# Two chained attention layers on one core: the output projection of layer 0 as seven block products into x1^T

## The chip, the cores and the metric

The kernel runs on one core of one Trainium2 chip. The metric is device time in microseconds (us) of one launch; lower is better. All data are fp32.

## The reference, cut to what matters

The input x is (8, 32, 32, 256): 8 batches of 1024 tokens with 256 channels. Layer 0 is attention with 4 heads, whose output projection is added to its input; layer 1 is a gated attention with one head of 32 channels on the result x1.

```python
# layer 0
q, k, v = split(xf @ W_qkv)                      # per head, 256 channels each
atten = softmax(einsum('bihd,bjhd->bijh', q, k) * C ** -0.5, axis=2)
res = einsum('bijh,bjhd->bihd', atten, v)        # heads side by side
x1 = res @ W_out + b_out + xf
# layer 1
f, g, h = x1 @ Wf + bf, x1 @ Wg + bg, x1 @ Wh + bh
b = softmax(einsum('bik,bjk->bij', g, f), axis=-1)
y = gamma * einsum('bij,bjd->bid', b, h) + x1
```

## The kernel before

**Algebra.** For each head the weights are folded once (`fold_weights`, L293): Wqk = Wq Wk^T and Wvo = Wv Wout, so that scores are (x Wqk) x^T and the head's contribution is softmax(..) x Wvo. The softmax is not shifted; the sum of the exponentials is divided out after the projection.

**Seven block products.** Most products are done as a 2 by 2 block scheme with seven instead of eight block products (`seven`, L234). It takes sums of blocks as operands, made by VectorE ahead (`sum_a` L204, `sum_b` L214), and uses three PSUM banks x, y, z in three tasks. `one` issues products 1, 6, 5 into x, y, z, ScalarE copies x to a tile e, and VectorE makes u = y + e. `two` adds product 2 to x and 7 to y; ScalarE takes result 11 from x, VectorE makes v = y + e and result 22 = z + v. `three` adds product 4 to y and 3 to z; VectorE makes results 21 = y + e and 12 = z + u. The adds are all on L264, the matmuls all on L247. In the trace the banks are `psx`, `psy`, `psz`, with `_q` for the queries and `_y` for the weighted values.

**Steps.** The work is a list of steps (L891), each a unit (a batch and head of layer 0, or a batch of layer 1) and one of two halves of 512 query columns. With batch b > 0, layer 1 of batch b-1 stands after head 1 of batch b; for the last batch it stands after head 3. The body of a step (L917 to L989) is a list of tasks, each with a place: `put(tasks, *places)`. The tasks are sorted by place, and this order is the program order of TensorE, VectorE and ScalarE (L870, a manual schedule): each engine takes its instructions strictly in that order. A layer-0 step i does

- its own scores (`scores`, L524): two groups of three tasks at places 0, 2, 4 and 6, 8, 10, exp on ScalarE;
- of step i-1: block sums of the exponentials (`sums`, L559, four operations of 128x1024 on VectorE), the column sums for the denominators (`first` and `second` in L582 to L600, a GpSimd all-reduce and two small DMAs that turn a row into columns), and the first two tasks of the weighted values (`products`, L608; places 5 and 9);
- of step i-2: the third task of the weighted values (place 1), `invert` (L604) and `project` (L629) at places 3 and 7;
- in the second half, the next head's queries (`queries`, L496) and their four block sums.

**The projection before** (`project`, L629) takes for each half eight matmuls of 128x128 by 128x256: the stationary operand is y (128 tokens at a time), the moving one is Wvo. The result has tokens in partitions, so that one VectorE operation multiplies by the inverse denominator (one number per partition) and adds to the rows of x1 (`rows1`, L648).

**Around it.** `residual` (L425) starts `rows1` as x + b_out on VectorE. Layer 1 needs x1 transposed: `turn_rows` (L357) moves 32x32 squares with DMAs on the queue of SyncE (SP) and transposes each square on VectorE (L382, L385); it does so for x of the next batch and for x1. For the last batch x1 is transposed by TensorE (`transpose_rows`, L342, called at L986). `queries_apart` (L687) makes f and g of layer 1 and spreads copies of them by DMAs from SP. `values` (L723) makes the value rows of layer 1 in four tasks, whose PSUM banks (pool `psm`, two buffers) VectorE empties (L729). After the last step the code from L1012 on finishes layer 1 of the last batch.

**Pools** (L866): `rows` has 4 buffers, `xT` 2, `m0` 1, `ps` six banks, `psm` two.

Of the kernel before, what the change touches and what calls it, by code (L numbers as in the profile page):

```python
# [16 lines left out]
P = 128  # L17
# [3 lines left out]
def kernel(  # L21
# [14 lines left out]
):  # L36

# [111 lines left out]
    bout_sb = const.tile([P, C], F32, tag="bout", name="bout_sb")  # L149
# [8 lines left out]
    def load_rest():  # L158
        with nc.allow_non_contiguous_dma(reason="small bias vectors, loaded once"):
            nc.sync.dma_start(bout_sb, b_out.partition_broadcast(P))  # L160
# [20 lines left out]
    wblocks = {}  # L181
# [52 lines left out]
    def seven(name, width, parts, matmuls, outs, tags, copy, after=None):  # L234
# [7 lines left out]
        def bank(k):  # L242
            banks[k] = tile_of("ps", [P, NB], f"ps{k}_{name}")[:, :width]
# [22 lines left out]
        def one():  # L266
            for k, number in (("x", 1), ("y", 6), ("z", 5)):
                bank(k)
                product(k, number, True)
            nc.scalar.copy(scratch("e"), banks["x"])  # L270
            add(shaped(scratch("u")), "y", sbs["e"])
# [19 lines left out]
    NARROW = dict(e="eh", u="uh", v="w")  # L291

    def fold_weights(h):  # L293
# [20 lines left out]
        def multiply(i, what):  # L314
# [13 lines left out]
            if i == 0:  # L328
# [4 lines left out]
                wblocks[h] = b_operands(blocks, sums)  # L333

# [22 lines left out]
    def turn_rows(b, src, dst, layer, scratch=None):  # L357

        Q = 32

        def end():
            if b not in dst:
                dst[b] = tile_of("xT", [P, CC, N], f"x{layer}T_{b}")
            return dst[b]

        def flat(t):
            return t.rearrange("p u n -> p (u n)").rearrange("p (s q) -> p s q", q=P)  # L370

        def move(a, c=None):
            to, rows_v = flat(end() if scratch is None else scratch()), flat(src[b])
            if c is not None:
                to, rows_v = to[:, ts(c, NT), :], rows_v[:, c::CC, :]
            for q in range(P // Q):
                nc.sync.dma_start(to[ts(q, Q), :, ts(a, Q)], rows_v[ts(a, Q), :, ts(q, Q)])

        def piece(k, c):
            to = end()[:, c, ts(k, NB)]  # L380
            if scratch is None:
                nc.vector.transpose(to, to)  # L382
            else:
                squares = scratch()[:, k, :].rearrange("p (t c q) -> p t c q", c=CC, q=P)
                nc.vector.transpose(to.rearrange("p (t q) -> p t q", q=P), squares[:, :, c, :])  # L385

        return (
            [partial(move, a, c) for a in range(P // Q)
             for c in ((None,) if scratch else range(CC))],
            [partial(piece, k, c) for k in range(NBLK) for c in range(CC)],  # L390
        )

# [32 lines left out]
    def residual(b):  # L425


        def piece(i):
            if i == 0:
                rows1[b] = tile_of("rows", [P, NT, C], f"x1_{b}")  # L430
            nc.vector.tensor_tensor(
                rows1[b][:, ts(i, 2), :], rows[b][:, ts(i, 2), :],
                bout_sb.unsqueeze(1).broadcast_to([P, 2, C]), ALU.add,
            )

        return [partial(piece, i) for i in range(NT // 2)]
# [40 lines left out]
    def values_tile(name):  # L477
        v = tile_of("v", [P, NT, CV], name)
        nc.gpsimd.memset(v[:, :, C : C + 1], 1.0)
        return v  # L480


    class Layer0:
        def __init__(self, b, h):
            self.b, self.h, self.name = b, h, f"{b}_{h}"
            self.p, self.y, self.r = {}, {}, {}
            self.products_of, self.pblocks = {}, {}
# [8 lines left out]
        def queries(self):  # L496
# [6 lines left out]
            def after():  # L503
                t = tile_of("qs", [P, 3, NBLK, HB], f"qs_{self.name}")
                q = self.q.rearrange("p c (k e i) -> p c e k i", k=NBLK, e=2)
                blocks = [q[:, c, e] for c in range(CC) for e in range(2)]
                sums = [blocks[1]] + [t[:, k] for k in range(3)]
                self.pieces = sum_b(sums, *blocks)
                self.blocks = b_operands(blocks, sums)

            def piece(k):
                self.pieces[k]()  # L512

# [7 lines left out]
                WIDE, nc.scalar.copy, after,  # L521
            ), [partial(piece, k) for k in range(4)]

        def scores(self, blk):  # L524
# [10 lines left out]
            for g in range(0, half, 2):  # L535
# [3 lines left out]
                def after(g=g, out=out):  # L539
# [8 lines left out]
                         self.blocks[number][:, blk, :])  # L548
# [10 lines left out]
        def sums(self, blk):  # L559
# [6 lines left out]
            def start():  # L566
# [4 lines left out]
                s2 = tile_of("s2", [P, half, HB], f"s2_{n}")  # L571
                s3 = tile_of("s3", [P, half, HB], f"s3_{n}")
                sums = [t[:, 1], s2, s3, t[:, 0]]
# [8 lines left out]
            def first():  # L582
                t = made["t"]
                made["m"] = m = tile_of("m0", [P, 2, 2, HB], f"m_{n}")
                tt(m, t[:, :, 0:2, :], t[:, :, 2:4, :], ALU.add)

            def second():
                m = made["m"]
                r = tile_of("rs", [P, 2, HB], f"rs_{n}")
                tt(r, m[:, :, 0, :], m[:, :, 1, :], ALU.add)  # L590
                tt(r[:, 0, :], r[:, 0, :], r[:, 1, :], ALU.add)  # L591
                t = tile_of("rb", [P, NB], f"rb_{n}")
# [9 lines left out]
            return [partial(piece, i) for i in range(4)], [first, second]  # L602

        def invert(self, blk):  # L604
            n = self.first + blk * HT
            nc.vector.reciprocal(inverse[:, n : n + HT], self.r[blk])
# [22 lines left out]
        def project(self, blk):  # L629

            b = self.b
# [501 lines left out]
```

## Time and profile before

| | |
|---|---|
| median of 3 runs | 2338.45 us (2338.1 to 2339.13) |
| profiled execution, its own time | 2338.61 us |
| its span, first to last instruction | 2336.7 us |
| TensorE matmuls, time in which one was under way | 2326.9 us |
| VectorE busy | 1481.7 us |
| ScalarE busy | 522.5 us |
| GpSimd busy | 211.5 us |
| data moved by DMA | 42.94 MB |
| granted TensorE clock | 0.999 |

Each fp32 matmul has two records in the trace, and records overlap: the mean record lasts 379 ns, but 16 records of the same kind take 3.47 us from the first's start to the next group's. VectorE records overlap as well, by less than a tenth of a microsecond. So lengths of stretches are best read from one start to the next.

### The profile page before, as it was taken

The page shows a single profiled execution, that of the slowest core. Times are in us where ns is not written, and L with a number is a line of the kernel's source. Part 1 is how long each engine was busy: PE and PEld are TensorE (multiplying, and loading weights), DVE is VectorE, ACT ScalarE, POOL GpSimd, SP SyncE. Part 2 cuts the span into 40 slices and gives each one's busy share as a digit, 9 for nine tenths or more (in the row PEclk, how much of TensorE's full clock was granted, in tenths as well). Part 3 has the DMA queues.
Part 4 walks back from the last instruction along what each step waited for, and adds up shares of the span by engine and source line. Part 5 has one row for each costly group of instructions (what it writes and reads, how often), then busy time and mean ns, then how long its engine had stood idle before and what let it go on. Part 6 is the DMA issues. An engine that isn't in the chain of part 4 may idle for free.

```text
span 2336.7 us, 26026 instructions
## 1 busy us (share of the span) xinstructions
PE 2326.9 (100%) x10394; PEld 1918.8 (82%) x10394; DVE 1481.7 (63%) x2398; ACT 522.5 (22%) x875; POOL 211.5 (9%) x79
## 2 busy tenths in 40 slices
PE   9999999999999999999999999999999999999999
PEld 7888888788878888788887888878888788888877
DVE  6667775377754767557774577645776457766635
ACT  2222222222221222212222122221222222222222
POOL 0111111011110111101111011110011101101110
PEclk9999999999999999999999999999999999999999
DMA  4000010100101001110011000110001100000100
GB/s 138 1 1 1 1 37 14 34 1 11 27 17 32 1 19 21 19 29 1 19 26 18 24 1 19 30 18 19 1 19 30 19 19 1 1 1 1 30 7 31
DMA packets 170257, 42.94 MB, mean 18 GB/s; under 512 B 158160, under 2 KB 163024, under 8 KB 170128
## 3 DMA queue, kind: packets, MB, share of 16 engines
q1 hardware_dynamic: 170128, 41.20, 8.0%
q8 instruction: 84, 1.38, 0.3%
q14 instruction: 45, 0.37, 0.1%
HBM read 13.37 MB, written 8.52 MB: 9 GB/s over the span
## 4 chain that ended last, share of the span: by engine, by line
PE 99%; DVE 1%; DMA 0%; issue 0%; ACT 0%
PE psy_y L247 14%; PE psy L247 14%; PE psx L247 9%; PE pa_l L834 9%; PE po L637 9%; PE psx_y L247 9%; PE psz_y L247 9%; PE psz L247 9%; PE psy_q L247 4%; PE psx_q L247 2%; PE psz_q L247 2%; PE pr_v_l L466 2%; PE ps_l L746 1%; PE pm_fg L703 1%; PE pwqk L318 0%; PE pwvo L318 0%
## 5 line engine op out<-in xcount | busy, mean ns | idle before, releaser
L593 POOL PARTITION_ALL_REDUCE rb<-rs x64 | 206.9, 3233 | 2046.6 <-DVE rs L591 2019.8
L247 PE MATMUL psx<-q,x0T 128*128 128x256 f32 x1024 | 263.6, 380 | 0.0
L247 PE MATMUL psy<-qs,xs 128*128 128x256 f32 x1024 | 263.0, 379 | 0.0
L247 PE MATMUL psz<-q,xs 128*128 128x256 f32 x1024 | 262.8, 379 | 0.0
L541 ACT ACTIVATE p<-p 128x1024 f32<-128x1024 f32 x128 | 135.3, 1057 | 554.8 <-DVE p L264 554.8
L247 PE MATMUL psy_y<-s,xt 128*128 128x256 f32 x1024 | 242.4, 380 | 0.1
L637 PE MATMUL po<-wvo,y 128*128 128x256 f32 x1024 | 241.9, 379 | 0.0
L247 PE MATMUL psx_y<-p,x 128*128 128x256 f32 x1024 | 241.9, 379 | 0.0
L834 PE MATMUL pa_l<-v_l,s_l 128*128 128x257 f32 x1024 | 232.1, 381 | 0.4 <-DVE v_l L729 0.4
L247 PEld LDWEIGHTS psx<-q,x0T 128*128 128x128 f32 x1024 | 194.0, 190 | 45.2 <-issue 21.0
L637 PEld LDWEIGHTS po<-wvo,y 128*128 128x128 f32 x1024 | 194.6, 190 | 39.5 <-issue 14.8
L834 PEld LDWEIGHTS pa_l<-v_l,s_l 128*128 128x128 f32 x1024 | 193.8, 190 | 36.6 <-issue 10.5
L247 PEld LDWEIGHTS psx_y<-p,x 128*128 128x128 f32 x1024 | 194.7, 190 | 34.0 <-issue 8.6
L247 PEld LDWEIGHTS psy_y<-s,xt 128*128 128x128 f32 x1024 | 191.9, 190 | 30.6 <-issue 2.4
L247 PEld LDWEIGHTS psy<-qs,xs 128*128 128x128 f32 x1024 | 194.5, 190 | 27.0 <-DVE qs L512 0.4
L247 PEld LDWEIGHTS psz<-q,xs 128*128 128x128 f32 x1024 | 194.7, 190 | 26.3
L264 DVE TENSOR_TENSOR u<-psy,e 128x512 f32<-128x512 f32 x128 | 88.4, 691 | 144.3 <-ACT e L270 73.4
L276 ACT ACTIVATE p<-psx 128x512 f32<-128x512 f32 x128 | 76.4, 597 | 413.7 <-PE psx L247 413.6
L264 DVE TENSOR_TENSOR v<-psy,e 128x512 f32<-128x512 f32 x128 | 87.8, 686 | 124.5 <-PE psy L247 124.5
L247 PE MATMUL psy<-qs,x0T 128*128 128x256 f32 x512 | 131.6, 380 | 0.7 <-DVE v L264 0.7
L648 DVE SCALAR_TENSOR_TENSOR x<-po,inverse,x 128x256 f32<-128x256 f32 x256 | 111.9, 478 | 31.3 <-PE po L637 22.4
L270 ACT COPY e<-psx 128x512 f32<-128x512 f32 x128 | 73.8, 576 | 257.8 <-PE psx L247 257.8
(120 smaller groups left out, 2839.8 us busy)
## 6 DMA issues: line engine op xcount, KB each, us to landing
out_dram<-x SPq DMA_DIRECT2D x15, 512.0 KB, 2.6
x<-in_x_dram SPq DMA_DIRECT2D x14, 512.0 KB, 4.6
x0T<-x SPq DMA_DIRECT2D x224, 32.0 KB, 1.9
fg<-x SPq DMA_DIRECT2D x112, 64.0 KB, 2.1
fg<-fg SPq DMA_DIRECT2D x56, 64.0 KB, 2.0
w<-in_L_conv_W_qkv_dram SPq DMA_DIRECT2D x4, 512.0 KB, 7.3
x<-in_x_dram SPq DMA_DIRECT2D x4, 256.0 KB, 4.8
w<-in_L_conv_W_qkv_dram SPq DMA_DIRECT2D x4, 256.0 KB, 6.4
```

The costliest lines, as they stand in the source:

```text
L247: nc.tensor.matmul(banks[k][:, ts(i, w)], lhsT=lhsT, rhs=rhs, start=first and n == 0, stop=True, skip_group_check=True,)
L264: nc.vector.tensor_tensor(dst, shaped(banks[k]), shaped(other), ALU.add)
L270: nc.scalar.copy(scratch("e"), banks["x"])
L276: copy(outs["11"](), shaped(banks["x"]))
L466: nc.tensor.matmul(pm[:, ts(j, C)], lhsT=src()[:, c, ts(2 * t2 + j, P)], rhs=w()[:, c, :], start=(c == 0), stop=(c == CC - 1),)
L541: exp(both, both)
L593: nc.gpsimd.partition_all_reduce(t, r.rearrange("p e i -> p (e i)"), P, bass_isa.ReduceOp.add)
L637: nc.tensor.matmul(pm[:, ts(j, C)], lhsT=self.y[blk][:, c, ts(2 * t2 + j, P)], rhs=folded[self.h][1][:, c, :], start=(c == 0), stop=(c == ...
L648: nc.vector.scalar_tensor_tensor(acc, pm[:, ts(j, C)], inverse[:, n : n + 1], acc, ALU.mult, ALU.add)
L703: nc.tensor.matmul(pm[ts(k, half)], lhsT=w[:, c, :], rhs=x1T_of[b][:, c, ts(k, NB)], start=(c == 0), stop=(c == CC - 1),)
L746: nc.tensor.matmul(pm, lhsT=self.f[ts(r, CK), ts(j0 + r, P)], rhs=self.g[ts(r, CK), ts(blk, NB)], start=True, stop=True,)
L834: nc.tensor.matmul(pm[:, : C + 1], lhsT=p[:, j, ts(ti, P)], rhs=v[:, j, : C + 1], start=(j == 0), stop=(j == NT - 1),)
```

## The change

The projection now computes Wvo^T times y^T, so that its result is x1 transposed, in seven block products of the same size (128x128 by 128x256) in the three tasks of `seven`. Its PSUM comes from the two `psm` banks (y and z share one). The denominators now lie along the free axis: `invert` writes its columns to DRAM as a row and reads that back into all partitions, and one VectorE operation multiplies the whole 128x1024 result by it. A DMA of GpSimd's queue then adds the product to x1^T in SBUF. x1^T starts as x^T + b_out, made by ScalarE. Rows of x1, needed for layer 1's output, are made from x1^T by 32x32 squares (`turn_back`), for all batches; TensorE's 16 transposes of the last batch go. The block sums of the queries are made per half. The key sums of the exponentials are in place, without the tiles s2 and s3. The next batch's squares are moved over two steps and transposed one step earlier than before. In the last step the queries of layer 1 move behind the last step, and the values there are spread between other products.

```diff
-    def seven(name, width, parts, matmuls, outs, tags, copy, after=None):
+    def seven(name, width, parts, matmuls, outs, tags, copy, after=None, two_banks=False):
...
         def bank(k):
-            banks[k] = tile_of("ps", [P, NB], f"ps{k}_{name}")[:, :width]
+            if not two_banks:
+                banks[k] = tile_of("ps", [P, NB], f"ps{k}_{name}")[:, :width]
+            elif k == "z":
+                banks[k] = banks["y z"][:, width : 2 * width]
+            else:
+                t = tile_of("psm", [P, NB], f"ps{k}_{name}")
+                banks["y z"], banks[k] = t, t[:, :width]
...
     def fold_weights(h):
...
+            else:
+                t4 = const.tile([P, 4, P], F32, tag=f"wo{h}", name=f"wo{h}")
+                sums = [t4[:, k, :] for k in range(4)]
+                blocks = [t[:, c, ts(e, P)] for e in range(CC) for c in range(CC)]
+                run(sum_a(sums, *blocks))
+                oblocks[h] = a_operands(blocks, sums)
...
+    def squares(dst, src, swap):
...
+        def move(a, c):
+            for q in range(P // Q):
+                to, rows_v = dst(), src()
+                if swap:
+                    nc.sync.dma_start(
+                        to[ts(q, Q), :, c, ts(a, Q)], rows_v[ts(a, Q), c, :, ts(q, Q)]
+                    )
...
+        def piece(k):
+            to = dst()
+            n = to.shape[1] * to.shape[2] // 4
+            flat = to.rearrange("p u v i -> p (u v) i")[:, ts(k, n), :]
+            nc.vector.transpose(flat, flat)
...
+    def turn_back(b):
...
+        return squares(end, lambda: x1T_of[b].rearrange("p c (n i) -> p c n i", i=P), True)
...
     def residual(b):
...
+        def piece(c):
+            if c == 0:
+                x1T_of[b] = tile_of("xT", [P, CC, N], f"x1T_{b}")
+            nc.scalar.activation(
+                x1T_of[b][:, c, :], xT_of[b][:, c, :], AF.Identity, bias=boutT_sb[:, c : c + 1]
             )
...
+        def query_sums(self, blk):
...
+                    t = tile_of("qs", [P, 3, HB], f"qs_{self.name}_{blk}")
+                    q = self.q.rearrange("p c (k e i) -> p c k e i", k=NBLK, e=2)
+                    blocks = [q[:, c, blk, e] for c in range(CC) for e in range(2)]
...
-            def first():
+            def add(k):
                 t = made["t"]
-                made["m"] = m = tile_of("m0", [P, 2, 2, HB], f"m_{n}")
-                tt(m, t[:, :, 0:2, :], t[:, :, 2:4, :], ALU.add)
...
+                if k == 1:
+                    made["r"] = tile_of("rs", [P, 2, HB], f"rs_{n}")
+                r = made["r"]
+                tt(r, t[:, :, 0, :] if k == 1 else r, t[:, :, k, :], ALU.add)
...
         def invert(self, blk):
             n = self.first + blk * HT
-            nc.vector.reciprocal(inverse[:, n : n + HT], self.r[blk])
+            inv = inverse[:, n : n + HT]
+            nc.vector.reciprocal(inv, self.r[blk])
+            if blk in self.rb:
+                return
+            line = tile_of("line", [1, NB], f"inv_{self.name}_{blk}")
+            with nc.allow_non_contiguous_dma(reason="columns turn into a row"):
+                nc.sync.dma_start(line.rearrange("o (t p) -> p (o t)", p=P), inv)
+            self.rb[blk] = t = tile_of("invb", [P, NB], f"invb_{self.name}_{blk}")
+            nc.sync.dma_start(t, line[0].partition_broadcast(P))
+
+        def invert_all(self, blk):
+            self.rb[blk] = t = tile_of("rs", [P, NB], f"invb_{self.name}_{blk}")
+            nc.vector.reciprocal(t, self.total[blk])
...
         def project(self, blk):
...
+            def piece(i):
+                if i == 0:
+                    y = self.y[blk]
+                    t = tile_of("yt", [P, 3, HB], f"yt_{n}")
+                    blocks = [y[:, c, ts(e, HB)] for c in range(CC) for e in range(2)]
+                    sums = [blocks[1]] + [t[:, k] for k in range(3)]
+                    made["l"] = sum_b(sums, *blocks)
+                    made["b"] = b_operands(blocks, sums)
+                made["l"][i]()
...
+            def add():
+                o = made["o"]
+                nc.vector.tensor_tensor(
+                    o, o, self.rb[blk].unsqueeze(1).broadcast_to([P, CC, NB]), ALU.mult
+                )
+                nc.gpsimd.dma_start(
+                    x1T_of[self.b][:, :, ts(blk, NB)], o, accum_op=ALU.add
+                )
...
-                    nc.sync.dma_start(self.g[q, ts(k, NB)], g)
+                    nc.gpsimd.dma_start(self.g[q, ts(k, NB)], g)
...
-        s=2, rows=4, xT=2, v=2, q=2, qs=2, xt=1, ss=1, s2=1, s3=1, m0=1, rs=1, rb=1,
-        y=2, e=2, u=2, w=1, eh=1, uh=1, st=2, r=8, line=4, ps=6, psm=2,
+        s=2, rows=3, xT=3, v=2, q=2, qs=2, xt=1, ss=1, m0=1, rs=1, rb=1,
+        y=2, yt=1, invb=1, e=2, u=2, w=1, eh=1, uh=1, eo=1, uo=1, st=2, r=8, line=4, ps=6, psm=2,
...
-            put([partial(u.invert, k)], 2.9 if l0 or blk == 1 else 1.9)
-            put(u.project(k), *((3, 7) if l0 else (2, 6) if blk == 0 else (3, 7)))
+            if nxt is None:
+                put([partial(u.invert_all, k)], 2.2)
+            put([partial(u.invert, k)], 3.4 if l0 else 2.7)
+            ysums, tasks, adds[i] = u.project(k)
+            put(ysums, *((1.1, 1.2, 1.3, 3.3) if l0 else (2.6, 2.7, 2.8, 3.1) if blk == 0 else
+                         (1.1, 1.2, 1.3, 2.1)))
+            put(tasks, *((3, 5.5, 7) if l0 else (5.2, 6, 7.2) if blk == 0 else
+                         (3, 5, 7) if nxt else (2.1, 3.9, 4.1)))
+            if nxt is None:
+                put(adds[i], 5)
+        if i - 1 in adds:
+            put(adds[i - 1], 0.5 if l0 or blk == 1 else 2.3)
...
-            put(sums[:2] + sums[3:], *((2.2, 3.2, 4.2) if l0 else (0.8, 2.2, 4.5)))
-            put(sums[2:3], 5.2 if l0 else 5.5)
-            put(keys, *((6.2, 8.2) if l0 else (7.6, 9.6)))
+            put(sums, *((2.1, 3.2, 4.2, 5.6) if l0 else (0.8, 2.2, 3.5, 5.5)))
+            put(keys, *((6.3, 6.6, 7.6, 8.7) if l0 else (6.3, 7.6, 8.3, 8.7)))
...
-        if l0 and a.h == 2 and blk == 1 and a.b + 1 < B:
-            moves, squares = turn_rows(a.b + 1, rows, xT_of, 0)
-            put(moves, *range(1, 9))
-        if l0 and a.h == HEADS - 1 and blk == 0 and a.b + 1 < B:
-            put(squares, 0.4, 1.4, 3.4, 4.4)
-            put(key_sums(a.b + 1), 5.4, 6.4, 7.2, 7.4)
+        if is_l0(nxt) and nxt[0].h == 2 and nxt[1] == 0 and nxt[0].b + 1 < B:
+            moves, turned = turn_rows(nxt[0].b + 1)
+            put(moves[:4], 1, 3, 5, 7)
+        if l0 and a.h == 2 and a.b + 1 < B:
+            if blk == 0:
+                put(moves[4:], 1, 3, 5, 7)
+            else:
+                put(turned, 0.7, 1.4, 2.4, 3.4)
+                put(key_sums(a.b + 1), 5.7, 6.4, 7.4, 8.3)
...
         if not l0 and blk == 0:
             put(a.values(), 0.9, 1, 3, 5, 8)
+            put(turned1, 2.5, 2.9, 4.2, 5.1)
         if nxt is None:
-            put(transpose_rows(B - 1, rows1, x1T_of, 1), 2.5, 4.5, 8.1, 8.2)
-            put(final.queries(), 2.4, 6.5, 9)
+            fg = final.queries()
+            moves, turned1 = turn_back(B - 1)
+            put(moves, *[9.1 + 0.1 * k for k in range(8)])
...
-    run(own[:1], s0[:1], prod[:1], p0[:1], s0[1:], prod[1:2], p0[1:2])
-    weave((prod[2:] + own[1:], 0, 1), (s1, 0.3, 0.7), (p1[:2], 0.55, 0.95), (p0[2:], 0.1, 0.9))
+    run(own[:1], prod[:1], fg, s0[:1], p0[:1], own[1:2], s0[1:], own[2:3], p0[1:2])
+    weave((prod[1:] + own[3:], 0, 1), (p0[2:], 0.1, 0.6), (turned1, 0.5, 1), (s1, 0.55, 0.95), (p1[:2], 0.75, 1))
```

## The prediction

> **What bounds the kernel now.** I read the page's busy shares and chain first, then the groups by shape, then the timeline of TensorE and VectorE through one batch. The page:
>
> ```profile
> PE 2326.9 (100%) x10394; PEld 1918.8 (82%) x10394; DVE 1481.7 (63%) x2398; ACT 522.5 (22%) x875; POOL 211.5 (9%) x79
> ...
> PE 99%; DVE 1%; DMA 0%; issue 0%; ACT 0%
> ```
>
> TensorE has work for all but 10 us, and the chain that ended last is TensorE from end to end: a matmul taken away is time taken away, as long as nothing comes late for the matmuls that stay. The other engines matter only through that. The groups by shape (busy us and mean ns of one behind the bar):
>
> ```profile
> L637 PE MATMUL po<-wvo,y 128*128 128x256 f32 x1024 | 241.9, 379 | 0.0
> L580 DVE TENSOR_TENSOR ss<-p 128x1024 f32<-128x1024 f32 x64 | 77.7, 1214 | 0.0
> L648 DVE SCALAR_TENSOR_TENSOR x<-po,inverse,x 128x256 f32<-128x256 f32 x256 | 111.9, 478 | 31.3 <-PE po L637 22.4
> L590 DVE TENSOR_TENSOR rs<-m 128x512 f32<-128x512 f32 x64 | 43.5, 680 | 0.0
> L591 DVE TENSOR_TENSOR rs<-rs 128x256 f32<-128x256 f32 x64 | 27.2, 425 | 2.2
> L264 DVE TENSOR_TENSOR y<-psz_y,u_y 128x256 f32<-128x256 f32 x64 | 27.2, 424 | 82.0 <-PE psz_y L247 82.0
> ```
>
> The first row is the projection, the others price what VectorE will do. Three steps of batch 4 (second half of head 2, both halves of batch 5's head 0), busy time per engine:
>
> ```profile
> 1320.31:1347.30 26.99, 26.97 (x112) 20.83 (x111) 19.61 (x29) 7.21 (x12) 0.38 (x1) 1.00 0.05 20
> 1408.56:1436.18 27.62, 27.62 (x129) 24.27 (x128) 19.65 (x32) 6.04 (x10) 3.41 (x3) 1.00 0.01 1
> 1436.18:1469.82 33.64, 33.64 (x144) 27.00 (x142) 25.24 (x41) 7.21 (x12) 3.11 (x2) 1.00 0.10 32
> ```
>
> Columns: length, then PE, PEld, DVE, ACT, POOL. PE fills each step; DVE, 70 to 75% full, is the one to watch. How close it runs shows where the scores' second task hands over to the third, with a projection task between:
>
> ```profile
> 1354.20 1.03 PE L247 MATMUL psy<-qs,xs 128*128 128x256 f32 x4
> 1355.07 1.89 PE L637 MATMUL po<-wvo,y 128*128 128x256 f32 x8
> 1356.79 1.03 PE L247 MATMUL psy<-qs,x0T 128*128 128x256 f32 x4
> ```
>
> ```profile
> 1355.27 0.69 DVE L264 TENSOR_TENSOR v<-psy,e 128x512 f32<-128x512 f32 x1 [0.68 <-PE psy L247]
> ```
>
> The third task's first product (1356.79) may start when v has read its bank (1355.96): 0.83 us to spare, because the projection's 1.72 us lie between.
>
> **What the Trainium skill says.** (1) "Trainium Kernel Development and Optimization", Performance Expectations: matmul busy time is a bad measure, since matmuls are pipelined. The trace agrees: a po record lasts 379 ns, but eight take 1.72 us, so I use distances between starts. (2) "VectorE: DVE Perf Modes", The TRN2 errata: an fp32 add of N columns takes (N+151)/0.96 ns. That gives 424 ns for 256 columns, and the trace has 424 to 425; so new VectorE operations can be priced from rows of their size. (3) "DMA: Bandwidth & Descriptors", Anatomy of one DMA: a GpSimd-issued DMA takes about 2.0 us plus its bytes at 436 GB/s. The accumulating DMA of 512 KB would take an estimated 3.2 us; the trace before has none of that queue. (4) "SBUF — State Buffer", Who interferes with whom: a VectorE operation with two SBUF inputs blocks, and is blocked by, a GpSimd instruction that reads SBUF. No row here shows it: the all-reduce (1346.92 to 1350.15) lies beside adds that read PSUM.
>
> **The change part by part.**
>
> *TensorE.* Eight products become seven of the same shape. Two tasks of four matmuls take 1.725 us each, so 0.431 us a matmul; 64 halves: **-27.6 us**. The last batch's 16 transposes go: they stood at 2258.16 (0.49 to the next start), 2263.85 (0.43) and 2271.28 (0.87): **-1.8 us**. The matmuls for f and g only move. No stage is added on TensorE. Gain if nothing comes late: 29.4 us.
>
> *VectorE.* Per half out: four L648 rows, 4 x 0.478 = 1.91 us. In: four sums of y (4 x 0.425 = 1.70), five adds from the banks (5 x 0.424 = 2.12), the 128x1024 multiply (1.21): 5.03. Denominator sums: 3 x 0.680 + 0.425 for 1.215 + 0.680 + 0.425, +0.15. Net +3.27, times 64 = 209 us. Query sums: eight of 0.425 for four of 0.687 per head, 32 heads, +21; residual to ScalarE (2 x 1.06 us a batch) -21; squares +3 (32 pieces for 28 of x1). Sum 1482 + 212 = 1694 us, 73% of the shorter span. By step: head 0's first half 19.65 - 2.73 - 1.91 + 5.03 + 0.15 + 1.70 = 21.9 of 27.2 us (81%), its second half 27.5 of 33.2 (83%). Head 2's second half (no projection falls there after batch 0, since two steps before is layer 1) takes the squares (4 x 0.70) and key sums (4 x 0.68) of the next batch: 19.61 + 5.5 - 1.05 + 0.15 = 24.2 of 27.0 (90%).
>
> *Order, plain step.* I laid the new order on the starts of the trace. An operation holds VectorE from its start to the next for 1.13 us (1024 columns), 0.60 (512) or 0.34 (256), 0.12 more if the next needs it. From the step's start TensorE does scores one (to 2.6), weighted values three (to 6.05), scores two (to 7.8), projection one (to 9.1), scores three. VectorE does u, multiply (to 3.75), two adds (the second ends 6.6), three y sums (to 7.85), v (8.0 to 8.7), 22 (to 9.3). The cover for v has shrunk to 1.30 us, and v still ends 0.4 us ahead; the third task's second product, at 9.97, needs 22 at 9.3. The projection's second product needs a y sum of 7.85 at 8.23. Later tasks have over 0.5 us. Cost **0**; it is what rival C takes away.
>
> *Head 2's second half.* Count from scores one of the second group (T = 1337.80). Before: u at T+1.98, then the sum and four query sums, v at T+6.50, needed at T+7.77. After: the query's last add, sum 1.13 and key sum 0.60 come first, so u at T+2.53; then u 0.60, three key-column sums and two key sums of 0.60, query sums 0.34+0.46+0.46+0.34: v at T+7.75, ends T+8.4. TensorE waits 0.65. The lag also meets the next step: its second product needs the bank that the add 21 frees. Before, that add ended at 1348.12 and the product started at 1348.16; after, about 0.5 late. 1.15 us in each of 7 batches: **+8.0** (0 to 16).
>
> *Layer 1's first half.* Value task three is followed at once by projection one, which needs both psm banks. In the trace that value task ends at 1545.21 and its bank is emptied at 1546.16; the projection fills 0.43 us of that with x, so 0.55 x 7 = **+3.9** (2 to 8).
>
> *Ends.* At the start four weight sums (0.29 each) stand ahead of two key sums on VectorE: **+1.0** (0 to 3; they wait for ScalarE's copy of Wvo). Last step: `invert_all` is a reciprocal of 512 columns. The trace has 168 ns for four columns and for one, so hardly over 1 ns a column, 0.7 us. f and g now wait for the last accumulation: the projection ends, adds and multiply take 2.2 us, the DMA 3.2 to 8, while TensorE has three products of 3.47 us and 1.8 us of f, g for the first half: 12.2 of cover. **+1.0** (0 to 5).
>
> *DMAs and queues.* The accumulation is bounded by a store of that size (2.6 us) and, reading, adding and writing, three times the bytes plus the fixed part, 5.6; I allow 8 and take 4. The next writer of its single buffer is ScalarE's copy in projection two, 13 us after the multiply (about 9 in layer 1's first half): hidden; without cover each microsecond over would stop ScalarE's exp behind it. On GpSimd's queue it stands after an all-reduce that ended 2 us earlier; the eight g copies there are followed by one due 20 us later. On SP, `invert` adds two DMAs behind one another (`st<-line` of 2 KB takes 2.1 us; allow 8 for both), needed 17 us later by the multiply. `turn_back` puts 32 moves of 0.65 us issue for 16 before; behind them stand the two inverse DMAs, and ahead of them the wait for the accumulation. 10 us of queue in steps with 17 us of slack: 0. Nor does the all-reduce meet the multiply: it ends about 0.5 us into a step, the multiply starts at 2.6.
>
> Sum against the profiled execution's own time (span 2336.7 plus 1.9 around it): 2338.6 - 27.6 - 1.8 + 8.0 + 3.9 + 1.0 + 1.0 = **2323.1 us**. That execution stands 0.2 above the runs' median; 2323 serves for both.
>
> **Rivals.** A (forecast): 2316 to 2333. B, *all hidden*: the tight handovers are met, since my lag of 0.5 to 0.65 us is smaller than one VectorE operation; 2338.6 - 29.4 = 2309, to 2316. For it: VectorE idles 20% or more in most steps. Against: the add that ended 0.04 us before its bank was needed. C, *slower*: the shortened cover between scores two and three. v is 0.4 us ahead; if one more 1024-column operation (1.13) is still running, because a y sum or an add from PSUM comes late, TensorE waits 0.73 us in each of some 50 layer-0 steps with a projection: +36, 2360. It turns the sign from about 0.3 us a step (29.4 - 13.9 = 15.5 over 50). For it: in-order VectorE 81 to 83% full; against: the layout above. D, *half of that*, or the accumulation over 9 us, so that ScalarE waits for the buffer in some steps: 2333 to 2343. That the change does less than it says: the diff issues seven products per half where eight stood, of one shape; 2 in 100.
>
> **Chances.** A 0.50, B 0.22, C 0.14, D 0.12, other 0.02. The range 2309 to 2340 takes A, B and two thirds of D (0.80) and leaves out C and the rest. Faster by over 0.2% (4.7 us, about what a measurement of this kernel can tell from no change): A, B and a little of D, 0.74; within 0.2%: the rest of D and the like, 0.12; slower: C, 0.14.
>
> **What would show it.** po's 1024 records must give way to 896 of the same length, and VectorE's busy time rise to about 1690. Right: waits of TensorE only in head 2's second half, the step after it, and before the projection's second product in layer 1; period of a batch 287.1 - 3.4 + 1.7 = 285.4. B: period 283.7. C: a wait at scores three in every step. Wrong altogether: ScalarE waiting for a DMA before its copy out of the projection, or VectorE stretched beside GpSimd.

## The result and the profile after

| | median us | runs | range |
|---|---|---|---|
| before | 2339.13 | 5 | 2338.1 to 2339.46 |
| changed | 2328.97 | 5 | 2327.4 to 2329.33 |

The ratio is 0.9957, with a 95% interval of 0.9942 to 0.9971. The kernel became 10.2 us faster where 15.4 were forecast: 6 us above the predicted time, inside the range and inside case A. The profiled execution took 2329.28 us, its span 2327.5 (before 2336.7), so the two traces have 9.2 us between them to explain.

The page of the changed kernel: busy time by engine, the chain by engine, and the adding DMA (KB each, us to landing).

```profile
PE 2305.0 (99%) x10250; PEld 1892.2 (81%) x10250; DVE 1655.6 (71%) x2963; ACT 585.0 (25%) x1015; POOL 317.8 (14%) x199
...
PE 3%; DMA 1%; ACT 0%; DVE 0%; issue 0%; ACTq 0%; DVEq 0%
...
x1T<-o POOLq DMA_DIRECT2D x64, 512.0 KB, 5.0
```

TensorE has 144 records fewer: 128 of the product saved and 16 of the transposes. It is still the bound, but the space around it grew from 9.8 us (2336.7 - 2326.9) to 22.5. The chain no longer helps: followed back from the end it breaks off after 4% of the span, near an adding DMA. The groups by shape (busy us and mean ns of one, then idle before):

```profile
L699 DVE TENSOR_TENSOR o<-o,invb 128x1024 f32<-128x1024 f32 x64 | 79.8, 1247 | 16.2 <-DMA invb<-inv 16.1
...
L255 PE MATMUL psy_o<-yt,wo 128*128 128x256 f32 x256 | 77.7, 385 | 4.4 <-DVE v_l L794 2.9 <-DVE u_o L272 1.1 <-DVE yt L690 0.4
L255 PE MATMUL psx_o<-y,wvo 128*128 128x256 f32 x256 | 76.3, 380 | 0.2 <-ACT e_o L278 0.2
L255 PE MATMUL psy_o<-y,wo 128*128 128x256 f32 x256 | 76.1, 379 | 0.0
...
L255 PE MATMUL psy_o<-yt,wvo 128*128 128x256 f32 x128 | 38.4, 382 | 0.5 <-DVE o L272 0.5
```

256 + 256 + 256 + 128 = 896 records of 379 to 385 ns stand for the 1024 of `po`. Where TensorE now waits, by what it waits for (us in total, times, longest):

```profile
PE psy L255 <- DVE v L272: 4.4, 8, 0.8
PE psy_y L255 <- DVE ss L612: 3.7, 6, 0.6
PE psy_o L255 <- DVE v_l L794: 2.9, 7, 0.4
...
PE psy_o L255 <- DVE u_o L272: 1.1, 7, 0.2
```

Before, after the start, the list had 0.7 us for v (twice) and 0.4 us for v_l (once), and nothing else. These lists count idle time against records whose ends are modelled, and understate. So I took every distance from one start on TensorE to the next and subtracted what the records between need (0.2158 us for each record of 256 columns, from the long undisturbed rows). Gaps over 0.12 us:

| place | gaps, us | beyond before, us |
|---|---|---|
| head 2's second half, second product of the weighted values, 6 batches | 0.78 (before 0.18) | 3.6 |
| there, scores three, 6 batches (and 0.23 in batch 0) | 0.71 (before none) | 4.5 |
| layer 1's first half, second product of the projection, 7 | 0.58 | 4.0 |
| there, second task of the projection, 7 | 0.32 | 2.2 |
| batch 1, head 2's first half, once | 0.93 | 0.9 |
| last two steps and end | 0.63, 0.56, 0.40, 0.38 (before 0.56) | 1.4 |
| start, up to the first plain step | | 0.4 |
| first records after each new wait, about 0.1 slower each | | 2.4 |
| together | | 19.4 |

29.4 - 19.4 = 10.0 against 9.2; the 0.8 that is left isn't assigned to a place.

In head 2's second half (batch 4) the two places on TensorE before, then on TensorE and VectorE of the changed kernel:

```profile
1330.64 1.89 PE L247 MATMUL psx_y<-p,x 128*128 128x256 f32 x8
1332.55 1.97 PE L247 MATMUL psy_y<-s,xt 128*128 128x256 f32 x8
...
1343.84 1.89 PE L247 MATMUL psy_y<-s,xt 128*128 128x256 f32 x8
1345.57 1.03 PE L247 MATMUL psy<-qs,x0T 128*128 128x256 f32 x4
```

```profile
1325.42 1.89 PE L255 MATMUL psx_y<-p,x 128*128 128x256 f32 x8
1327.93 1.97 PE L255 MATMUL psy_y<-ss,xt 128*128 128x256 f32 x8 [0.62 <-DVE ss L612]
...
1339.21 1.89 PE L255 MATMUL psy_y<-p,xt 128*128 128x256 f32 x8
1341.65 1.13 PE L255 MATMUL psy<-qs,x0T 128*128 128x256 f32 x4 [0.55 <-DVE v L272]
...
1344.35 1.03 PE L255 MATMUL psy<-qs,xs 128*128 128x256 f32 x4
```

```profile
1323.51 1.22 DVE L612 TENSOR_TENSOR ss<-p 128x1024 f32<-128x1024 f32 x1
1324.64 0.70 DVE L394 STREAM_TRANSPOSE x0T<-x0T 128x512 f32<-128x512 f32 x1
1325.27 0.65 DVE L272 TENSOR_TENSOR v_q<-psy_q,e_q 128x512 f32<-128x512 f32 x1
1325.96 0.69 DVE L272 TENSOR_TENSOR q<-psz_q,v_q 128x512 f32<-128x512 f32 x1
1326.57 1.22 DVE L612 TENSOR_TENSOR ss<-ss,p 128x1024 f32<-128x1024 f32 x1
...
1339.71 0.68 DVE L433 TENSOR_TENSOR xs<-x0T 128x512 f32<-128x512 f32 x1
1340.31 0.68 DVE L619 TENSOR_TENSOR rs<-rs,ss 128x512 f32<-128x512 f32 x1
1340.91 0.68 DVE L272 TENSOR_TENSOR v<-psy,e 128x512 f32<-128x512 f32 x1
...
1343.97 0.68 DVE L272 TENSOR_TENSOR p<-psy,e 128x512 f32<-128x512 f32 x1
```

From `psx_y` to `psy_y` it was 1.91 us and is 2.51; from the later `psy_y` to scores three it was 1.73 us and is 2.44. The second weighted product needs the block sum `ss`, which ends at 1327.79; a transposed square (1324.64) and the query's two adds stand ahead of it. Scores three needs v, which ends at 1341.59; a key sum (1339.71) and a key-column sum stand right ahead of it. VectorE has no idle time in either stretch. In the windows the step is 28.40 us long (26.99 before), and VectorE is busy for 22.90 of them (columns: length, PE, PEld, DVE, ACT, POOL, clock, DMA share, GB/s):

```profile
1315.08:1343.48 28.40, 27.23 (x111) 20.72 (x110) 22.90 (x37) 7.21 (x12) 0.05 (x1) 1.00 0.16 56
```

Layer 1's first half on TensorE, for batch 3:

```profile
1249.21 1.89 PE L493 MATMUL pr_v_l<-wh_sb,x1T 128*128 128x256 f32 x8
1250.94 0.59 PE L255 MATMUL psx_o<-y,wvo 128*128 128x256 f32 x2
1251.95 0.70 PE L255 MATMUL psy_o<-yt,wo 128*128 128x256 f32 x2 [0.41 <-DVE v_l L794]
...
1252.91 0.59 PE L255 MATMUL psx_o<-y,wvo 128*128 128x256 f32 x2
1253.66 0.70 PE L255 MATMUL psy_o<-yt,wo 128*128 128x256 f32 x2 [0.15 <-DVE u_o L272]
```

The first wait is the forecast one: value task three has just filled a `psm` bank, and v_l on VectorE must empty it. The second wasn't forecast: u of the projection comes late for task two.

Two things befall VectorE's new multiply. In layer 1's second half it runs beside GpSimd's all-reduce, and in head 2's first half it waits for the inverse row (batch 1):

```profile
402.94 3.22 POOL L625 PARTITION_ALL_REDUCE rb<-rs  x1 [16.30 <-issue]
404.75 1.49 DVE L699 TENSOR_TENSOR o<-o,invb 128x1024 f32<-128x1024 f32 x1
...
436.48 1.23 DVE L699 TENSOR_TENSOR o<-o,invb 128x1024 f32<-128x1024 f32 x1 [4.15 <-DMA invb<-inv]
```

The first happens seven times and makes the multiply longer (1492 to 1496 ns; the other 57 take 1215 to 1226); TensorE doesn't wait behind it. The second happens six times, for 2.0 to 4.1 us; only in batch 1, where it is longest, is v behind it late: that is the 0.93 us of the table.

### The profile page after: what moved, and what is told of

It is laid out like the page before. It is cut to its first block, busy times and chain, and to the rows that moved or that the text cites. A ratio compares the mean times of both kernels' runs of the same rounds, so it can differ in the third digit from the quotient of the medians.

```text
span 2327.5 us, 27263 instructions
## 1 busy us (share of the span) xinstructions
PE 2305.0 (99%) x10250; PEld 1892.2 (81%) x10250; DVE 1655.6 (71%) x2963; ACT 585.0 (25%) x1015; POOL 317.8 (14%) x199
## 5 line engine op out<-in xcount | busy, mean ns | idle before, releaser
L255 PE MATMUL psy_y<-p,xt 128*128 128x256 f32 x1024 | 241.9, 379 | 0.0
L255 PEld LDWEIGHTS psy_y<-p,xt 128*128 128x128 f32 x1024 | 194.6, 190 | 26.5
L702 POOL DMA_DIRECT2D x1T<-o x64 | 78.0, 1219 | 431.1 <-DVE o L699 310.1
L255 PE MATMUL psy_y<-ss,xt 128*128 128x256 f32 x512 | 121.4, 380 | 3.7 <-DVE ss L612 3.7
L255 PE MATMUL psz_y<-ss,xt 128*128 128x256 f32 x512 | 121.0, 379 | 0.0
L255 PE MATMUL psz_y<-ss,x 128*128 128x256 f32 x512 | 120.9, 379 | 0.0
```

The lines of the kernel that those rows point to most:

```text
L255: nc.tensor.matmul(banks[k][:, ts(i, w)], lhsT=lhsT, rhs=rhs, start=first and n == 0, stop=True, skip_group_check=True,)
L702: nc.gpsimd.dma_start(x1T_of[self.b][:, :, ts(blk, NB)], o, accum_op=ALU.add)
```

## The experiments

Theory: TensorE is the bound everywhere, and the missing gain is the sum of local waits, each made by the place of one or two tasks in the written order; move those, and the gain comes back up to B's 2309. Rivals: the waits only move on when one is taken away, because VectorE is full (then C is near and no reordering helps); or the loss is contention with the new DMA traffic. The runs were made on four chips, and the kernel before took 2338.57 to 2339.03 us (medians) on them; so differences to the changed kernel of half a microsecond tell nothing.

**The eighth product put back**, to see what a product is worth in the changed kernel. The first of the seven is issued twice; the second issue overwrites the first.

```diff
             for k, number in (("x", 1), ("y", 6), ("z", 5)):
                 bank(k)
+                if two_banks and k == "x":
+                    product(k, number, True)
                 product(k, number, k != "z" or not two_banks)
```

> The first of the seven products of each projection is issued twice (the second overwrites the first), so that TensorE does eight products as before; all else stays. Theory (TensorE bounds, each product is 0.431 us of path): 64 x 0.431 = 27.6 us more, less about 3 us where the extra product fills the wait for the bank in layer 1's first half: 2353 to 2357 us, well above the kernel before. Rival (TensorE is no longer the bound in most steps, VectorE is): under 15 us more, below 2344 us.

2351.08 us (2349.92 to 2351.78), ratio to before 1.0051 (1.0036 to 1.0067); 22.1 above the changed kernel, a little below what was expected. Where TensorE waited ahead of the projection's second product (0.58 and 0.56) only 0.14 of the gap is left, eight times: 3.4 us of waits are filled. The single waits of 0.93 and 0.63 are gone too: 27.6 - 3.4 - 1.6 = 22.6. The matmul term of the sum holds, and TensorE is the bound.

**The key sums and one square moved.** The next batch's key sums go from head 2's second half to head 3's first, the third square from place 2.4 to 3.3.

```diff
-                put(turned, 0.7, 1.4, 2.4, 3.4)
-                put(key_sums(a.b + 1), 5.7, 6.4, 7.4, 8.3)
+                put(turned, 0.7, 1.4, 3.3, 3.4)
+        if l0 and a.h == HEADS - 1 and blk == 0 and a.b + 1 < B:
+            put(key_sums(a.b + 1), 5.7, 6.4, 7.4, 8.3)
```

> The four key sums go from head 2's second half to head 3's first half (same places), and the third piece of squares from place 2.4 to 3.3, behind the sum that TensorE waits for. Theory (VectorE's queue in head 2's second half, 90% full, is what makes TensorE wait there): the 0.78 us ahead of the weighted values' second product and the 0.71 us at scores three, with the slower records after them 1.6 us in 6 batches, go: 9 to 10 us less, 2319 to 2320 us. Rival (head 3's first half has as little room, about 92% with the key sums): the waits move there, 2326 to 2330 us.

2317.99 us (2317.75 to 2318.82), ratio 0.9911 (0.9898 to 0.9925): 11.0 better than the changed kernel. The gaps in head 2's second half are 0.18 and none, and none appear in head 3. Those gaps are worth 3.6 + 4.3 + 0.6 for the slower records; the single waits of 0.93 and 0.63 are gone as well. The 0.93 is no fixed cost: of all the traces only three others have a gap there, of 0.40, 0.22 and 0.20. It follows the wait of VectorE's multiply for the inverse row in batch 1: 4.15 us in the changed kernel, 3.61, 3.43 and 3.41 in those three, 3.2 or less in the rest. Both moves were in one run; so one of them was run alone.

**The square alone.**

```diff
-                put(turned, 0.7, 1.4, 2.4, 3.4)
+                put(turned, 0.7, 1.4, 3.3, 3.4)
```

> The changed kernel with the third of the four square transposes moved from place 2.4 to 3.3 in head 2's second half; the key sums stay where the change put them. This separates the two moves that one experiment made together. Theory (each wait has its own cause: the square at 2.4 delays the block sum that the weighted values' second product needs, the key sums delay v of scores three): the gap ahead of that second product falls from 0.78 to 0.18 in six batches, the 0.71 ahead of scores three stays, 2329.0 - 3.6 - some 0.6 for the slower records after each wait = about 2325. Rival (the square's delay is handed on along VectorE's queue to v, and the key sums only add to it): the 0.71 falls too, to 0.1 to 0.4, and the time is 2322 to 2323. Other rival (TensorE, no longer held at the second product, reaches scores three earlier while VectorE is no earlier there, so the wait only moves): the second wait grows to 1.2 to 1.3 and the time stays at 2328 to 2329.

2324.06 us (2323.85 to 2324.41), ratio 0.9936 (0.9919 to 0.9952): 4.9 better than the changed kernel. On TensorE, batch 4:

```profile
1322.68 1.89 PE L255 MATMUL psx_y<-p,x 128*128 128x256 f32 x8
1324.59 1.96 PE L255 MATMUL psy_y<-ss,xt 128*128 128x256 f32 x8
...
1335.88 1.89 PE L255 MATMUL psy_y<-p,xt 128*128 128x256 f32 x8
1338.31 1.13 PE L255 MATMUL psy<-qs,x0T 128*128 128x256 f32 x4 [0.55 <-DVE v L272]
```

From `psx_y` to `psy_y` it is 1.91 us now, 2.51 in the changed kernel; the second wait is as it was (0.71 in all six). Of the 4.9 us, 3.6 are the six shorter gaps; the 0.63 in the last batch is gone too, and the 0.93 is 0.40. So the two waits have separate causes: the square makes the first, and the key sums, taken with the experiment before, the second. Neither rival holds; the lag isn't handed on.

**Value task three earlier in layer 1's first half**, so that its bank is empty when the projection begins.

```diff
-            put(a.values(), 0.9, 1, 3, 5, 8)
+            put(a.values(), 0.9, 1, 3, 3.5, 8)
```

> The third value task of layer 1's first half moves from place 5 to place 3.5, so that the weighted values (5.2 us of TensorE) lie between it and the projection. Theory (the projection waits there for a psm bank that VectorE empties, and its second task then follows too closely): the 0.58 and 0.32 us and the slower records after them, 1.1 us in each of 7 batches, go: 7.7 us less than the changed kernel's 2329, so 2321 us. Rival (ScalarE's copy out of the projection waits for the accumulating DMA that reads the single buffer m0, and the banks come free late for that reason): the wait only moves to the projection's third task, 2328 to 2329 us.

2322.93 us (2321.49 to 2323.66), ratio 0.993 (0.9916 to 0.9943): 6.0 better. The 0.58 is gone in all seven layer-1 steps; the 0.32 stays, so it isn't a consequence of it. In the last batch the wait for the adding DMA grew from 0.63 to 1.17. The 0.32 on TensorE and VectorE, in batch 3:

```profile
1248.16 0.59 PE L255 MATMUL psy_o<-yt,wo 128*128 128x256 f32 x2
1248.59 0.59 PE L255 MATMUL psy_o<-y,wo 128*128 128x256 f32 x2
...
1249.77 0.70 PE L255 MATMUL psy_o<-yt,wo 128*128 128x256 f32 x2 [0.15 <-DVE u_o L272]
```

```profile
1249.29 0.42 DVE L272 TENSOR_TENSOR u_o<-psy_o,e_o 128x256 f32<-128x256 f32 x1 [1.39 <-PE psy_o L255]
```

u reads the y half, written by 1248.16's product. It starts at 1249.29, after the z half's product (1248.59), which lies in the same bank: it waited for both. ScalarE's copy e, which u reads too, isn't the reason: it ended at 1248.73. That is read from these times. Two separate banks weren't tried, and in the program the halves are also one tile; so whether the bank or the program's order by tiles demands the wait stays open. With tasks one and two back to back there is no cover for that.

**The projection's tasks apart in layer 1's first half.**

```diff
-            put(tasks, *((3, 5.5, 7) if l0 else (5.2, 6, 7.2) if blk == 0 else
+            put(tasks, *((3, 5.5, 7) if l0 else (5.2, 7.1, 8.1) if blk == 0 else
```

> Only the projection's second and third tasks in layer 1's first half move, to 7.1 and 8.1, the second behind 3.5 us of weighted values. Theory (the add u waits until the bank that y and z share is written, and the second task follows too closely for that): the 0.32 us and the slower record after it go in 7 batches, and the 0.6 us that the last batch waited for the accumulation, 3 to 4 us less than the changed kernel, 2325 to 2326 us; the 0.58 us ahead of the projection's second product stay. Rival (the 0.32 us only follow from the 0.58 us ahead of them): no change in the rest, and the fourth value task now waits for a bank, 2329 to 2331 us.

2326.08 us (2325.5 to 2326.55), ratio 0.9945 (0.9932 to 0.9959): 2.9 better. The 0.32 is gone, the 0.58 stays, and a gap of 0.19 appears ahead of value task four.

**One 1024-column operation more on VectorE**, rival C's mishap brought about: a reduction into an unused number, ahead of v, in each layer-0 step with a projection.

```diff
+        if l0 and is_l0(two):
+            put([partial(nc.vector.tensor_reduce, junk, xT_of[a.b][:, 0, :1024], op=ALU.add, axis=AX.X)], 1.35)
```

> VectorE gets one more operation in every layer-0 step with a projection (50 steps): a reduction of 1024 columns of x^T into an unused number, placed behind the first three y sums, ahead of v. My layout gives v 0.4 us of room there, so that 1.13 us more make TensorE wait about 0.57 to 0.73 us at scores three in each of the 50 steps: 29 to 36 us more, 2358 to 2366 us. Rival (VectorE idles nearly 30% of the span, and the idle time takes it up): under 5 us more, below 2334 us.

2345.45 us (2344.17 to 2346.31), ratio 1.0028 (1.0016 to 1.004): 16.5 slower than the changed kernel, less than expected. TensorE:

```profile
1360.61 0.59 PE L255 MATMUL psy_o<-y,wo 128*128 128x256 f32 x2
1361.68 1.13 PE L255 MATMUL psy<-qs,x0T 128*128 128x256 f32 x4 [0.47 <-DVE v L272]
```

The gap is 0.64 us (1.07 less 0.43), near C's 0.73, but it comes in 25 steps, the first halves, and not in 50: in second halves a task of the next head's queries stands between scores two and three and covers v. **With 512 columns** in the same place (`:512` for `:1024`):

> As the run with 1024 more columns, but with 512: 0.60 us of VectorE in each of 50 layer-0 steps. The longer operation made TensorE wait 0.64 us in the 25 steps that have no query task there. Theory (a fixed room of about 0.4 to 0.5 us ahead of v, and all that exceeds it is waited for): 0.1 to 0.2 us in 25 steps, 2 to 6 us more than the changed kernel, 2331 to 2335 us. Rival (each VectorE operation ahead of v costs in proportion): half of the 16.5 us of the longer one, 2337 us.

2332.76 us (2331.84 to 2333.54), ratio 0.9974 (0.9962 to 0.9985): 3.8 slower, with a gap of 0.10 in 25 steps. The room of v in a plain first half follows twice: 1.13 - 0.64 = 0.49 and 0.60 - 0.10 = 0.50 us. C's price was real; its trigger didn't occur in the change, and its places were half as many.

**The inverse row later**, to separate two DMAs. In layer 1's first half the row of inverses is written to DRAM (512 single numbers) while the product is added to x1 transposed.

```diff
-            put([partial(u.invert, k)], 3.4 if l0 else 2.7)
+            put([partial(u.invert, k)], 3.4 if l0 else 2.7 if blk else 5.3)
```

> In layer 1's first half the reciprocal of the denominators, and with it the DMA that writes 512 single numbers to DRAM, moves from place 2.7 to 5.3, away from the accumulating DMA. Theory (the two slow each other): ScalarE and VectorE no longer wait there for the accumulation, which lands after about 5 us as elsewhere. Rival (it is slow there for another reason): they wait as before, 9.7 us and more after its issue. The time is not the question: the multiply of the next step may wait for the inverse, 2329 to 2340 us.

2326.71 us in a single run, 2.3 below the changed kernel's median. Who waited for the adding DMA, and its time to landing, changed kernel first:

```profile
  ACT o L284: 13.2, 3
  DVE o L272: 6.9, 3
...
DMA to landing us min/median/max: 5.0/5.0/12.9
```

```profile
  ACT o L284: 1.9, 1
...
DMA to landing us min/median/max: 5.0/5.0/6.6
```

In the changed kernel the adding DMA takes 9.7 to 12.9 us in these seven steps, beside the scatter, and at most 6.0 elsewhere; apart from the scatter none takes over 6.6. So contention between DMAs is real, but of TensorE's waits it explains at most the 0.63 in the last batch, which is not in this trace. The other waits of TensorE in head 2's second half and in layer 1 are unchanged. The multiply now waits for the later row in 13 steps, up to 3.6 us, and TensorE nowhere for that, so that the time came out below the 2329 to 2340 expected.

**All moves together**: value task three, key sums, square, tasks apart, and two rows for the last step:

```diff
-                         (1.1, 1.2, 1.3, 2.1)))
+                         (1.1, 1.2, 1.3, 2.1) if nxt else (0.3, 0.35, 0.4, 1.9)))
...
-                         (3, 5, 7) if nxt else (2.1, 3.9, 4.1)))
+                         (3, 5, 7) if nxt else (1.1, 2.1, 4.1)))
```

> The third value task at 3.5, key sums in head 3's first half and the third piece of squares at 3.3, and two more: in layer 1's first half the projection's second and third tasks at 7.1 and 8.1 (the second behind the weighted values, so that the add u from the bank that y and z share has 3.4 us of cover), and in the last step y sums at 0.3 to 0.4 and projection tasks at 1.1, 2.1, 4.1. Theory (the waits are separate and each costs what its gap shows): 2318 less 7 x 1.1 less 0.8 in the last step, 2309 to 2311 us, no wait of TensorE over 0.2 us between the start and the tail. Rival (the accumulating DMA, 9.7 us or more in layer 1's first half, is the next to be late): 0.4 to 1.2 us a batch stay, 2313 to 2317 us.

2312.45 us (2311.62 to 2312.75), ratio 0.9887 (0.987 to 0.9903), just above what was expected: 0.19 to 0.85 was left ahead of value task four, where ScalarE's copy of the projection was held by the adding DMA. **Value task four behind the projection** was meant to take that away:

```diff
-            put(a.values(), 0.9, 1, 3, 3.5, 8)
+            put(a.values(), 0.9, 1, 3, 3.5, 8.2)
```

> As the combination of all moves (2312.5 us), with the fourth value task of layer 1's first half at 8.2, behind the projection's third task, so that 0.86 us more lie between ScalarE's copy out of the projection and the value task that takes its bank. Theory (that copy, late by the accumulating DMA, is what the 0.2 to 0.85 us ahead of the value task wait for): 2 to 3 us less, 2309.5 to 2311 us, the wait gone or under 0.1 us. Rival (the bank comes free with the last adds only): the wait grows, 2313 to 2316 us.

A miss: 2318.93 us (2318.12 to 2319.52), 6.5 slower than without the move, ratio to before 0.9916 (0.9902 to 0.9929). TensorE, in layer 1 of batch 3:

```profile
1250.27 0.59 PE L255 MATMUL psy_o<-yt,wo 128*128 128x256 f32 x2
1251.97 0.70 PE L255 MATMUL psy_o<-yt,wvo 128*128 128x256 f32 x2 [1.10 <-DVE o L272]
```

Value task four had been the work between the projection's second and third task. Without it task three waits for VectorE's add that reads the same bank, 1.26 us in each of seven batches.

**All moves, and the inverse row later** instead (the two diffs above, value task four back at 8):

> The best version so far (2312.45) with the inverse denominators moved from place 2.7 to 5.3 in layer 1's first half, so that the row of inverses isn't written to memory while the product is being added to x1 transposed. Theory (the waits of 0.19 to 0.85 ahead of the fourth value task come from the late adding DMA, since ScalarE's copy stands behind it): they fall to 0.19 or less in all seven layer-1 steps, 2312.45 - 1.3 = about 2311. Rival (the copy is late by ScalarE's own queue, and the DMA only by chance): they stay, 2312.5. Rival (the inverse row comes too late for the multiply of the next step, which then holds VectorE for 3.5 us as seen with that move alone, and now v behind it is late): new waits of 0.5 or more in layer 1's second half or the step after, 2313 to 2317.

2310.41 us (2309.9 to 2311.4), ratio 0.9876 (0.986 to 0.9893). The page's busy line, and the waits that the trace lists for TensorE after the start:

```profile
PE 2299.4 (100%) x10250; PEld 1893.2 (82%) x10250; DVE 1655.2 (72%) x2963; ACT 585.5 (25%) x1015; POOL 317.9 (14%) x199
```

```profile
PE psy L255 <- DVE v L272: 0.3, 1, 0.3
PE ps_l L811 <- DVE fg L736: 0.2, 1, 0.2
```

What was left ahead of value task four is 0.19 in each of the seven batches, so the longer waits there did come from the DMA. The median is 28.6 us below before (2339.03 on the same chip), of the 29.4 that the saved matmuls are worth, with as many instructions on VectorE as the changed kernel has. This is the best version. A second buffer for the product (`m0`), the other way to loosen the adding DMA, wasn't tried.

## Why the prediction was right, and where it wasn't

- **TensorE, -27.6 and -1.8: right.** 144 records fewer of unchanged length; putting the product back costs 22.1, and 5.0 of waits go with it.
- **Plain steps at 0: right.** No gap at scores three in any first half, but for the 0.93 in batch 1; v's room was 0.5 us where 0.4 was laid out.
- **Head 2's second half, +8.0: right in sum by luck, wrong in one of its two places.** The 0.65 at scores three came as 0.71, by the order laid out: u at T+2.54 and v at T+7.74 (T is 1333.17), where T+2.53 and T+7.75 were written. The 0.5 in the next step did not come: the product I named starts at 1344.35, the add that was to hold it ends at 1344.65, so it doesn't wait for that add. I had read a cause into two times that agreed within 0.04 us. In its place stands 0.60 ahead of the second weighted product; that 3.6 us came where 3.5 had been put is chance. I had counted the four squares in the step's busy time and never laid their places against the block sum; the square at 2.4 falls exactly ahead of it. With 6 batches and the slower records: 3.6 + 4.5 + 0.7 = 8.8.
- **Layer 1's first half, +3.9: the step that failed.** The wait for the bank was right (0.58 for 0.55; the two times named there give 0.52). Missing was the second wait, 0.32: the working lays no time for u there and so puts it at nothing. y and z share a bank, and u waits for both. And each wait costs about 0.1 more, because the first records after it follow at a wider distance (0.53 us for a product from 1251.95, 0.43 for the one behind it). 4.0 + 2.2 + 1.4 = 7.6, which is 3.7 of the 6 us missed. In all the forecast put 13.9 us of waits, and 19.4 came; the range was wide enough for that.
- **DMAs "hidden, 13 us": right for the median, wrong at the edge.** The adding DMA landed in 5.0 us where 4 was taken and an estimate from the Trainium skill ("DMA: Bandwidth & Descriptors", Anatomy of one DMA) gave 3.2; the measurement decides. In layer 1's first half I named 9 us of cover and allowed 8, each DMA by itself; beside the scatter it took 9.7 to 12.9. That cost 0.63 once. The inverse pair was allowed 8: after the write alone SP waited 8.4 on average (531.0 us in 63 waits). In head 2's first half of batch 1 its reciprocal is at 413.38, the write is issued at 420.62, behind moves of the next batch's squares, the read at 432.28, and the multiply starts at 436.48. That is 23 us where the working has 10 us of queue and 17 us of slack; it cost the 0.93.
- **The signs of "wrong altogether" were too strong.** Both came: ScalarE waited for the adding DMA ahead of its copy in three of layer 1's first halves (13.2 us), and the multiply met the all-reduce in seven steps, where the prediction says that the two don't meet. Neither costs TensorE anything but the 0.63, so the mechanism of the forecast stands beside them.
- **Ends: +1.0 and +1.0, measured 0.4 and 1.4** (0.63 of it the adding DMA's). The reciprocal of 512 columns was taken as 0.7 us, from one and four columns at 168 ns each:

```profile
2252.54 3.34 DVE L653 RECIPROCAL invb<-rb 128x512 f32<-128x512 f32 x1
```

  It took 3.34. What hid it were the products of layer 1 beside it, not its size.
- **VectorE at 1694 us, measured 1655.6.** I summed durations of records that overlap: 1.21 against 1.13 from start to start, 0.68 against 0.60, 0.42 against 0.34. At 565 more instructions that is about 565 x 0.08 = 45 us counted twice, more than the 38 that are missing.
- **Period of a batch:** 285.4 forecast, 286.15 measured, 283.65 with nothing lost.
- **The rivals.** B was what the products are worth, and the schedule kept it away, not VectorE's load: with the same operations reordered the time is 2310.4. C was priced nearly right per place (0.64 for 0.73) and twice too often. D's long DMA exists, but in seven steps, and ScalarE waited for it in three.

## What to carry to other kernels

When work is moved into an in-order queue, lay each moved instruction on the times of the step and ask who stands behind it; a step's busy share (80% here) tells nothing of that, and one square 0.9 places too early cost 3.6 us. A task between a product and the next user of its bank is cover: before moving it, name what takes its place. Halves of a bank that are written by different products were one buffer here to the reader that waits.

## What the runs showed of the hardware

- VectorE's reciprocal is slow per column: 3344 ns for 128x512 (one operation), against 680 for an add of that shape.
- The adding DMA of 512 KB on GpSimd's queue keeps GpSimd busy for 1.22 us and lands after 5.0 (median); beside a scatter of 512 single numbers, after 9.7 to 12.9 in seven steps.
- TensorE's first product after a wait is followed by the next about 0.1 us later than in a running row (0.53 us from 1251.95, 0.43 from 1252.48).
- VectorE's multiply of 128x1024, both inputs in SBUF, took 1492 to 1496 ns in the seven places where it overlapped GpSimd's all-reduce, and 1215 to 1226 in the other 57 (the mean of 1247 mixes the two). Operations with an input in PSUM were not longer beside the all-reduce (418 to 425 ns on average for 128x256, as elsewhere). In the run with the inverse row later the multiply no longer overlaps it, and none takes over 1226.
